# Keys and values of the next group at other places of a group's slots, and other places for the steps behind the projection, in an attention and mixture-of-experts kernel

## Chip, cores and metric

The kernel runs on one core of a Trainium2 chip. The metric is the device time of one execution in microseconds (us). Before the change it is 1366.93 us, the median of three runs (1366.15 to 1367.98).

## The reference

The input x is 8 sequences of 512 rows with 256 numbers each, all fp32. Two blocks follow each other, each inside a "sandwich" of two layer norms.

```
x = x + layernorm(attention(layernorm(x)))
x = x + layernorm(ffn(layernorm(x)))

attention: q = x @ wq + bq + pe      16 heads of 128: 4 groups of 4 heads
           k = x @ wk + bk + pe      one key head for each group
           v = x @ wv + bv           one value head for each group
           softmax(causal(q @ k.T / sqrt(128))) @ v, then @ wo

ffn:       softmax over 64 experts, the 6 best of each row, at most 64 rows for each expert,
           silu(rows @ w_gate) * (rows @ w_up) @ w_down, weighted and summed;
           plus one shared expert on all rows
```

Mean and variance of a layer norm are over the 256 numbers of a row.

## The kernel before

**Units and slots.** The attention is cut into 128 units: 8 sequences ("batches"), 4 groups of heads, 4 units for a group. Unit k holds two blocks of 64 queries for each of the group's four heads, one from the first half of the sequence and one from the second, four score tiles in all. A loop over k (L1520) writes the work of all engines in order; what one pass of the loop issues is called slot k here. b = k // 16 is the batch and s = k % 16 the slot within it; "first" to "fourth" slot means k % 4 = 0 to 3. The order on each engine is the order in which the program issues (a manual schedule): an instruction that waits holds up all that is behind it on its engine, and a DMA that waits holds up all that is behind it in the queue of the engine that issues it. Two such queues matter here, that of SyncE (SP) and that of GpSimd (POOL).

**What a slot does.** `scores(k, q)` (L571) multiplies queries by the keys kt of the group (TensorE, PE: psc, L580), VectorE (DVE) adds the mask and finds the extreme (L584), ScalarE (ACT) takes the exponential with its sum (L588). `weigh(k)` (L591) takes the reciprocal on DVE (recip, L594) and scales on POOL (e, L598). In the next slot `turned` (L612) transposes the weights in blocks of 32 on DVE (eb, L616), writes them to DRAM by four DMAs of SP (ex_d, L620), and `read_turned` (L625) reads them back in another order (et, L629): this completes the transposition. Two slots after the scores `mix` (L652) multiplies them by the values v (pav, L665). In the second slot of each group it does four units' remaining products in banks called rest and more (L704), and for units of a second slot the read of et is issued after it (L1590), in other slots early.

**Queries.** Pairs of heads are made by a product with seven factors instead of eight (`ask` L479, `ask_sum`, `answer`, `ask_rest`, `ask_fourth`, `answer_fourth`): banks pq_front and pq_back in the first and third slots, "third" (L527) in the second and fourth.

**Keys and values of the next group.** `keys` (L374) is a product of two weights tiles with 512 columns (pk, L378), and DVE adds bias and positions (kt, L380). `values(b, g, n)` (L382) makes half n of the values (pv, L390), which ACT copies to v, and for n = 0 in part to w as well. `group_step(k)` (L399) says when: keys in the second slot, half 0 of the values in the third, half 1 in the fourth. It is called at the end of a slot (L1632), but for second slots up to unit 96 between `projections_behind` and `mix` (L1587), that is, right behind "third" and ahead of rest on PE. Slots 2 and 3 of batch 0 are special (L1582).

**Banks.** The score tiles, third, rest, more and some tiles of the feed-forward part share three PSUM banks (pool ps_s); pk, pv, pq, pav, psg, pg and others share three more (ps_m). A product waits until the last reader of the bank's former tile is done.

**The feed-forward part behind it.** While batch b is in the attention, the rows of batch b - 1 go through the output projection and the feed-forward part. `feed_forward(b - 1)` (L1260) gives a table of steps with a place each, a slot s and a side. In the order of a slot the sides are A and B behind `weigh`, with `projections` between them in some slots, M ahead of group_step and mix, and D at the end, ahead of the last call of group_step. Places such as "4M" are slot 4, side M. The steps that matter:
- copies: for batches 1 to 5 `combine` (L805) on POOL, six additions, gives o, the projected rows.
- scales(o), scales(xt): `norm_scales` (L84): four bn_stats, four bn_aggr and one addition on DVE, then a power on POOL (rs_o, rs_f).
- residual_sums: a shift on DVE from rs_o (L105), four scalings of o on ACT (L109), four additions to x on POOL (L1287); for batch 5 the scaling is on DVE.
- store: x to DRAM by POOL's queue (x_d, L1290).
- rows: the second layer norm into xg (DVE L118, ACT L109), turn: its transposition.

The rows of x live in two buffers, so the rows of batch b + 1 (`load_x`, L188, on SP's queue, issued behind the et read of slot 6) go where those of batch b - 1 were. Their moments (st_a) are taken in slot 7, normalised in slot 8. `cross` (L770), four additions on POOL, prepares a seven-factor product of the projection and is issued at the start and at the end of third slots; its products are ps and pc (L783).

Of the kernel before, what the change touches and what calls it, by code (L numbers as in the profile page):

```python
# [22 lines left out]
NI = T // P  # L23
# [22 lines left out]
LATE_UNITS = (EARLY + 1) * NH  # L46

@with_exitstack
def sandwich_kernel(ctx, tc, x, wq, bq_t, wkv, bk_t, bv, wo, gate_wt, w_gate, w_up, w_down,
# [107 lines left out]
    with ExitStack() as part:  # L157
# [216 lines left out]
        def keys(b, g):  # L374
            s = seqs[b]
            pk = bank([P, T], f"pk_{b}_{g}")
            for c in range(NC):
                nc.tensor.matmul(pk, lhsT=wkv_sb[:, c, g, 0, :], rhs=s["xnt"][:, c, :], start=c == 0, stop=c == NC - 1)  # L378
            kt = s["kt"][g] = p2.tile([D, T], F32, tag="kt", name=f"kt_{b}_{g}")
            nc.vector.scalar_tensor_tensor(kt, pk, bk_sb[:, g : g + 1], pe_sb, ALU.add, ALU.add)  # L380

        def values(b, g, n):  # L382
            s = seqs[b]
            if n == 0:
                s["v"][g] = p2.tile([P, NI, D], F32, tag="v", name=f"v_{b}_{g}")
                s["w"][g] = p2.tile([P, 2, D], F32, tag="w", name=f"w_{b}_{g}")
            pv = bank([P, 2, D], f"pv_{b}_{g}_{n}")
            for i in range(2):
                for c in range(NC):
                    nc.tensor.matmul(pv[:, i, :], lhsT=s["xnt"][:, c, ts(2 * n + i, P)], rhs=wkv_sb[:, c, g, 1, :],  # L390
                                     start=c == 0, stop=c == NC - 1, skip_group_check=True)
            on_act(s["v"][g][:, ts(n, 2), :], pv)
            if n == 0:
                on_act(s["w"][g][HALF:, :, :], pv[:HALF, :, :])
                on_act(s["w"][g][:HALF, 1, :], pv[HALF:, 0, :])
                if b > EARLY:
                    nc.gpsimd.memset(s["w"][g][:HALF, 0, :], 0.0)

        def group_step(k):  # L399

            b, n = divmod(k, NH)
            g, step = n // QPG + 1, n % QPG
            b, g = (b, g) if g < G else (b + 1, 0)
            if b == B:
                return
            if step == 1:
                keys(b, g)
            if step >= 2:
                values(b, g, step - 2)

        def units_of(k):
# [438 lines left out]
        def projections_behind(k):  # L850
            c = crossing(k)
            if c:
                add_up(c[0], 0)
                across(c[0])
# [194 lines left out]
        def gate_up(key):  # L1049
            l = pairs[key]  # L1050
            pgu = bank([P, 2, F], f"pgu_{key}")
            for c in range(2):
                for e in range(2):
                    nc.tensor.matmul(pgu[ts(e, CAP)], lhsT=l["gxt"][:, c, ts(e, CAP)],
                                     rhs=l["wgu"][:, e, :, c, :], start=c == 0, stop=c == 1)
            l["hid"] = p4[0].tile([P, F], F32, tag="xhid", name=f"hid_{key}", bufs=2)
            nc.scalar.activation(l["hid"], pgu[:, 0, :], AF.Tanh, scale=0.5)
            l["pgu"] = pgu

        def gate_up_hidden(key):  # L1060
            l = pairs[key]
            pgu = l.pop("pgu")
            nc.vector.scalar_tensor_tensor(l["hid"], l["hid"], 1.0, pgu[:, 0, :], ALU.add, ALU.mult)
            nc.vector.scalar_tensor_tensor(l["hid"], l["hid"], 0.5, pgu[:, 1, :], ALU.mult, ALU.mult)

        def turn_hidden(key):
            l = pairs[key]
            pt = ps_s.tile([P, 2, P], F32, tag="s", name=f"pth_{key}")
            cols = l["hid"].rearrange("s (p c) -> s c p", c=2)
            for c in range(2):  # L1070
                nc.tensor.transpose(pt[:FC, c, :], cols[:, c, :], ident)
            l["ht"] = p3.tile([FC, 2, P], F32, tag="ht", name=f"ht_{key}")
            on_dve(l["ht"], pt[:FC])
# [186 lines left out]
        def feed_forward(b):  # L1260
# [14 lines left out]
            def scales(src, name):  # L1275
                l["scales"] = norm_scales(tiles_of(src), f"{name}{b}")
# [42 lines left out]
            def go(which, n=1):  # L1319
                return lambda: [next(l[which]) for _ in range(n)]  # L1320

            steps = {
                "2D": copies, "3M": lambda: scales(l["o"], "o"), "4A": residual_sums,
                "5M": lambda: scales(xt, "f"), "5B": store, "6A": rows,
                "6M": turn, "7A": shared_gate, "7B": go("f"), "8A": gate,
                "8D": go("r"), "9D": go("r"),
            }
            def choice_behind(steps):
                choose, then = steps.pop("8D"), steps.get("9A", lambda: None)
                return steps | {"9A": lambda: (choose(), then())}  # L1330

            if b < B - 2:
                steps |= {"3D": steps.pop("2D"), "4M": steps.pop("3M"), "5A": steps.pop("4A"),
                          "5D": steps.pop("5M"), "6B": steps.pop("5B")}
            if b == B - 2:
                steps["6D"] = steps.pop("6M")
            if b < B - 2:
# [1 line left out]
            if b < EARLY:  # L1339
# [8 lines left out]
                steps = choice_behind(steps)  # L1348
# [15 lines left out]
            def down_late():  # L1364
# [3 lines left out]
            steps = choice_behind(steps) | {  # L1368
                "10A": go("r"), "10B": mark, "10D": gather_rows, "11D": lambda: gate_up("late"),
                "12A": lambda: gate_up_hidden("late"), "12D": lambda: turn_hidden("late"), "13A": down_late,  # L1370
            }
# [148 lines left out]
        for k in range(NK):  # L1520
# [61 lines left out]
            if k == 2:  # L1582
                group_step(2)
                group_step(3)
            projections_behind(k)
            if k % NI == 1 and k < LATE_UNITS:
                group_step(k)  # L1587
            if k >= 2:
                mix(k - 2)
            if 0 <= k - 1 < NK - 2 and k % NI == 1 and k <= LATE_UNITS + 1:  # L1590
# [25 lines left out]
            if s == 2 and b:  # L1616
                behind = feed_forward(b - 1)
# [10 lines left out]

            if s in ((6, 8, 9) if b == EARLY + 1 else (10,) if b <= EARLY else ()):
                next(ahead)()  # L1630
            if k not in (2, 3) and (k % NI != 1 or k >= LATE_UNITS):
                group_step(k)  # L1632
            twice = active and k > EARLY * NH + NH
            if twice and not finishing:
# [101 lines left out]
```

## Time and profile before

| what | value |
|---|---|
| median of 3 runs | 1366.93 us |
| the profiled execution | 1366.87 us |
| its span, first to last instruction | 1365.2 us |
| busy PE, DVE, POOL, ACT | 1312.4, 926.4, 662.5, 586.0 us |
| granted TensorE clock | 0.998 |
| batches 1 to 4 start at (PE, unit 16 b) | 145.3, 296.3, 446.6, 596.4 us |

The last row is the start of the first score product of each batch in the trace. A row of the waits names the engine, the tile and line that waited, who ended the wait, the total in us, how often, and the longest. A row of the timeline gives start and length in us, engine, line, operation, output and inputs, how many instructions are merged, and in brackets the idle time of that engine ahead of it with what ended it; DMA rows of a queue (SPq) are the times of issue. All matmuls are fp32 and each product of the code shows as two or more MATMUL records.

### The profile page before, as it was taken

The numbers are of one execution on the slowest core, as the hardware profiler recorded it, in microseconds if no ns is written. First come the engines' busy times: TensorE is split into PE (matmuls) and PEld (weight loads), VectorE is DVE, ScalarE is ACT, GpSimd is POOL, SyncE is SP. The second block draws the span as 40 slices with busy tenths as digits, with TensorE's granted clock in tenths as the row PEclk, the third lists the DMA queues.
The fourth block names the chain that finished last, engine by engine and source line by source line (L and its number), as shares of the span: only waits on it lengthen the run. The fifth ranks groups of instructions, "written<-read, shape, count | busy, mean of one in ns | idle before, by whom it ended". The sixth has DMA issues, their size and how long they took to land. (4 is left out here: it accounts for less than half of the span.)

```text
span 1365.2 us, 22004 instructions
## 1 busy us (share of the span) xinstructions
PE 1312.4 (96%) x6746; PEld 997.1 (73%) x6746; DVE 926.4 (68%) x2955; ACT 586.0 (43%) x1777; POOL 662.5 (49%) x1090
## 2 busy tenths in 40 slices
PE   8999999999899999999999999999999999999997
PEld 6777776877778876787678876877666676777774
DVE  5575677877787678777787769766656444567545
ACT  3444455344544454444534454433444344444423
POOL 4555453436543563446443554345545445477711
PEclk9999999999999999999999999999999999999999
DMA  8676667666666657675765656678999889777711
GB/s 265 176 228 206 201 173 223 200 201 199 184 217 203 194 178 231 187 224 166 212 201 176 195 179 192 187 219 279 307 287 284 249 241 303 177 243 260 212 38 71
DMA packets 160437, 285.54 MB, mean 209 GB/s; under 512 B 17292, under 2 KB 123437, under 8 KB 160317
## 3 DMA queue, kind: packets, MB, share of 16 engines
q1 hardware_dynamic: 122893, 212.14, 52.0%
q0 software_dynamic: 13328, 36.05, 8.8%
q10 hardware_dynamic: 24096, 35.92, 8.4%
q8 instruction: 55, 0.90, 0.3%
q14 instruction: 65, 0.53, 0.1%
HBM read 168.44 MB, written 115.61 MB: 208 GB/s over the span
## 5 line engine op out<-in xcount | busy, mean ns | idle before, releaser
L598 POOL TENSOR_SCALAR e<-e,recip 128x512 f32<-128x512 f32 (+1 forms) x504 | 245.0, 523 | 436.6 <-DVE recip L594 384.8
L588 ACT ACTIVATE e<-e,least 128x32 f32<-128x32 f32 (+1 forms) x504 | 258.5, 514 | 243.1 <-DVE least L584 223.3
L580 PE MATMUL psc<-kt,qt 128*128 128x32 f32 (+15 forms) x1024 | 274.8, 406 | 17.8 <-DVE least L584 10.8
L584 DVE CUSTOM_DVE_ANT_0 e<-psc,mask 128x32 f32<-128x32 f32 (+1 forms) x504 | 205.4, 430 | 110.9 <-PE psc L580 108.1
L665 PE MATMUL pav<-et,v 128*128 128x256 f32 (+1 forms) x1044 | 258.3, 387 | 18.0 <-DMA et<-ex_d 15.6
L665 PEld LDWEIGHTS pav<-et,v 128*128 128x128 f32 (+1 forms) x1044 | 190.3, 191 | 65.8 <-issue 21.1
L674 ACT ACTIVATE ao<-pav,bv_sb 128x256 f32<-128x256 f32 x207 | 89.4, 471 | 332.3 <-PE pav L665 313.6
L580 PEld LDWEIGHTS psc<-kt,qt 128*128 128x128 f32 x1024 | 162.2, 191 | 66.2 <-DVE least L584 31.8
L616 DVE STREAM_TRANSPOSE eb<-e 128x1024 f32<-128x1024 f32 (+1 forms) x252 | 197.6, 822 | 12.6 <-DMA ex_d<-eb 6.3
L588 ACT ACTIVATION_READ_ACCUMULATOR e<-e,least 128x1 f32 x504 | 94.3, 187 | 0.0
L1091 POOL DMA_INDIRECT y_d<-dd,idx x32 | 51.0, 1595 | 86.6 <-ACT e L588 39.5
L783 PEld LDWEIGHTS pc<-set,crossed 128*128 128x128 f32 x640 | 77.2, 192 | 3.1 <-POOL crossed L777 0.9
L783 PE MATMUL pc<-set,crossed 128*128 128x128 f32 x640 | 78.2, 275 | 0.0
L433 PE MATMUL pq<-xnt,wq_sb 128*128 128x256 f32 x320 | 75.5, 380 | 0.0
L477 PE MATMUL pq_back<-rows_joined,heads 128*128 128x256 f32 x264 | 71.3, 379 | 0.0
L390 PEld LDWEIGHTS pv<-wkv_sb,xnt 128*128 128x128 f32 x512 | 66.0, 192 | 5.8 <-ACT w L121 1.3
L390 PE MATMUL pv<-wkv_sb,xnt 128*128 128x128 f32 x512 | 67.7, 276 | 1.6 <-ACT w L121 1.1
L433 PEld LDWEIGHTS pq<-xnt,wq_sb 128*128 128x128 f32 x320 | 59.2, 190 | 9.9 <-issue 1.5
L783 PEld LDWEIGHTS ps<-set,ao 128*128 128x128 f32 x480 | 59.5, 192 | 8.0 <-issue 2.4
L477 PEld LDWEIGHTS pq_back<-rows_joined,heads 128*128 128x128 f32 x264 | 50.2, 190 | 16.2 <-issue 8.2
L378 PE MATMUL pk<-xnt,wkv_sb 128*128 128x512 f32 x128 | 60.2, 593 | 0.3 <-ACT xnt L121 0.3
L783 PE MATMUL ps<-set,ao 128*128 128x128 f32 x480 | 60.5, 276 | 0.0
(303 smaller groups left out, 2174.0 us busy)
## 6 DMA issues: line engine op xcount, KB each, us to landing
ex_d<-eb SPq DMA_DIRECT2D x504, 160.0 KB
et<-ex_d SPq DMA_DIRECT2D x126, 640.0 KB
wgu<-in_w_gate ACTq DMA_DIRECT2D x32, 352.0 KB
wgu<-in_w_up ACTq DMA_DIRECT2D x32, 352.0 KB
wd<-in_w_down ACTq DMA_DIRECT2D x32, 352.0 KB
set<-wc_d SPq DMA_DIRECT2D x20, 512.0 KB
set<-ws_d SPq DMA_DIRECT2D x20, 384.0 KB
y<-y_d POOLq DMA_DIRECT2D x10, 512.0 KB, 6.2
```

The costliest lines, as they stand in the source:

```text
L378: nc.tensor.matmul(pk, lhsT=wkv_sb[:, c, g, 0, :], rhs=s["xnt"][:, c, :], start=c == 0, stop=c == NC - 1)
L390: nc.tensor.matmul(pv[:, i, :], lhsT=s["xnt"][:, c, ts(2 * n + i, P)], rhs=wkv_sb[:, c, g, 1, :], start=c == 0, stop=c == NC - 1, skip_gro ...
L433: nc.tensor.matmul(pq[:, n, :, :], lhsT=wq_sb[g][:, c, ts(2 * pair + n, D)], rhs=seqs[b]["xnt"][:, c, :].rearrange("p (u v) -> p u v", v=P ...
L477: nc.tensor.matmul(out, lhsT=factor[0], rhs=factor[1], start=first, stop=last, skip_group_check=True)
L580: nc.tensor.matmul(psc[:, :w], lhsT=halves[k // 2][:, at, :, :].rearrange("d h t -> d (h t)"), rhs=seqs[b]["kt"][g][:, :w], start=True, st ...
L584: nc.vector.tensor_tensor_reduce(out=e, in0=psc[:, :w].rearrange("p (c t) -> p c t", t=BS), in1=mask[:, T - w :].rearrange("p (c t) -> p c ...
L588: nc.scalar.activation(e, e, AF.Exp, bias=l["least"][:, q : q + 1], scale=-1.0, accum_out=l["total"][:, q : q + 1])
L598: engine.tensor_scalar(e, e, recip[:, q : q + 1], 1.0, ALU.mult, ALU.mult)
L616: nc.vector.transpose(eb[:, :, first : first + count, :, :].rearrange("p a j r t -> p j a r t"), weighed[k % 2][:, end - count : end, :, : ...
L665: nc.tensor.matmul(out, lhsT=keys_, rhs=weights, start=first and at == 0, stop=last and at == len(some) - 1, skip_group_check=True)
L674: nc.scalar.activation(result_of(k, n), out, AF.Identity, bias=bias)
L783: nc.tensor.matmul(bank_[:, n, :], lhsT=a, rhs=w, start=pair == 0 and n == 0, stop=pair == 1 and n == len(factors[0]) - 1, skip_group_chec ...
```

## The change

`group_step`: for units 4 to 95 the steps within a group are mapped so that keys are made in the first slot, half 0 of the values in the second, nothing in the third, half 1 in the fourth, and every call is at the end of the slot. For the batches whose steps the second edit covers (steps of batches 0 to 5), scales(o) goes from 4M to 4A, residual_sums from 5A to 4M, scales(xt) from 5D to 5A, and store from 6B to 5B.

```diff
@@ group_step
             b, g = (b, g) if g < G else (b + 1, 0)
             if b == B:
                 return
+            if NI <= k < LATE_UNITS:
+                step = (1, 2, 0, 3)[step]
             if step == 1:
                 keys(b, g)
-            if step >= 2:
+            if 2 <= step <= 3:
                 values(b, g, step - 2)
@@ feed_forward
             if b < B - 2:
-                steps |= {"3D": steps.pop("2D"), "4M": steps.pop("3M"), "5A": steps.pop("4A"),
-                          "5D": steps.pop("5M"), "6B": steps.pop("5B")}
+                steps |= {"3D": steps.pop("2D"), "4A": steps.pop("3M"), "4M": steps.pop("4A"),
+                          "5A": steps.pop("5M")}
@@ the loop over k
             projections_behind(k)
-            if k % NI == 1 and k < LATE_UNITS:
-                group_step(k)
             if k >= 2:
                 mix(k - 2)
@@
-            if k not in (2, 3) and (k % NI != 1 or k >= LATE_UNITS):
+            if k not in (2, 3):
                 group_step(k)
```

## The prediction

> **What bounds the kernel now.** The page first. TensorE (PE) is busy in 96% of the span:
>
> ```profile
> span 1365.2 us, 22004 instructions
> ...
> PE 1312.4 (96%) x6746; PEld 997.1 (73%) x6746; DVE 926.4 (68%) x2955; ACT 586.0 (43%) x1777; POOL 662.5 (49%) x1090
> ```
>
> Its work is the same after the change, so only its idle time can go, 52.8 us in all. The view of the waits, for PE alone, says what ended it:
>
> ```profile
> PE pav L665 <- DMA et<-ex_d: 15.6, 16, 2.8
> PE psc L580 <- DVE least L584: 10.8, 12, 1.2
> PE psc L580 <- DVE qt L512: 6.4, 4, 1.7
> PE psg L1214 <- DVE qt L512: 3.3, 4, 1.0
> ...
> PE pav L665 <- DVE kt L380: 1.7, 4, 0.4
> ```
>
> The same view over batches 1 to 4 (145.3 to 746.9 us) gives 7.7 us in 8 waits for least, and all of the two qt rows and of the kt row: a pattern that returns in each batch. The timeline places it. I take batch 2, whose slots 4 to 10 start on PE at 328.85, 334.25, 343.68, 354.38, 365.02, 374.89 and 384.29:
>
> ```profile
> 334.03 1.89 POOL L598 TENSOR_SCALAR e<-e,recip 128x512 f32<-128x512 f32 x4 [4.46 <-DVE recip L594]
> ...
> 336.25 1.04 POOL L99 TENSOR_TENSOR rs_o<-ve_o,mhalf 128x4 f32<-128x4 f32 x1 [0.34 <-DVE ve_o L97]
> 336.39 1.02 PE L580 MATMUL psc<-kt,qt 128*128 128x448 f32 x2 [0.83 <-DVE least L584]
> ...
> 338.11 1.88 PE L378 MATMUL pk<-xnt,wkv_sb 128*128 128x512 f32 x4
> ...
> 342.11 2.78 POOL L1287 TENSOR_TENSOR x<-x,o 128x256 f32<-128x256 f32 x4
> ...
> 342.87 0.43 DVE L89 BATCH_NORM_STATS2 st_f<-x 128x6 f32<-128x256 f32 x1 [0.93 <-POOL x L1287]
> ...
> 346.12 0.59 PE L580 MATMUL psc<-kt,qt 128*128 128x384 f32 x1 [1.09 <-DVE least L584]
> ```
>
> Slot 4 is only 5.40 us of PE work, and DVE ends it with the moments of o; so in slot 5 PE waits 0.83 us for a bank that DVE has not read. At the end of slot 5 DVE waits 0.93 + 3 x 0.26 us for POOL's additions to x; so PE waits 1.09 in slot 6. Then the queues, each from the timeline of its engine (SP, POOL, DVE, PE):
>
> ```profile
> 352.19 0.34 SPq L629 DMA_DIRECT2D et<-ex_d  x1
> 358.22 0.40 SPq L188 DMA_DIRECT2D x<-in_x  x1
> 358.66 2.07 SPq L144 DMA_DIRECT2D exr_d<-xb_f  x4
> 360.77 2.87 SPq L620 DMA_DIRECT2D ex_d<-eb  x4
> ```
>
> ```profile
> 352.62 0.80 POOL L1290 DMA_DIRECT2D x_d<-x  x1
> ```
>
> ```profile
> 362.69 1.41 DVE L89 BATCH_NORM_STATS2 st_a<-x 128x6 f32<-128x256 f32 x4 [3.60 <-DMA x<-in_x]
> ...
> 366.87 1.57 DVE L616 STREAM_TRANSPOSE eb<-e 128x768 f32<-128x768 f32 x2 [0.92 <-DMA ex_d<-eb]
> ```
>
> ```profile
> 365.02 2.38 PE L580 MATMUL psc<-kt,qt 128*128 128x32 f32 x8 [1.60 <-DVE qt L512]
> ...
> 370.06 1.98 PE L1214 MATMUL psg<-xt,sg_sb 128*128 128x512 f32 x4 [0.94 <-DVE qt L512]
> ```
>
> This is one chain. The store of x (L1290) is issued at 352.62 and lands at 358.14; the next batch's rows go into that buffer, so their load stands at the head of SP's queue until 358.22, with eight writes behind it. DVE waits 3.60 us for the rows, reads the bank of "third" only after that, and PE loses 1.60 at the start of slot 8 and 0.94 within it.
>
> **The change part by part.** PE does the same instructions, so the gains and costs are waits. The sum is made against the profiled execution: 1366.87 us (span 1365.2 and 1.67 around it); the median of the runs is 1366.93, so 0.06 apart.
>
> *The store of x, from 6B to 5B.* On POOL it passes four cross operations and weigh(38). It follows rs_f: with the times found below, issue at 344.9, and with the same 5.5 us it lands near 350.5. The x load then waits for the last reads of x in slot 6 (351.9) and for the et read ahead of it, so it is issued near 352.4 instead of 358.22. It takes 4.4 us (358.22 to 362.6 before), to 356.8; DVE wants the rows when recip of slot 7 is done, near 358.4. Both waits of slot 8 go: 6.4 + 3.3 = **9.7 us** in batches 1 to 4. In batch 5 PE has no such wait.
>
> *Moments of o to 4A, additions to 4M, moments of x to 5A.* By hand from 333.95, where recip of slot 4 ends: moments of o 1.79 us to 335.74, gxt 0.34 to 336.1. Now shift_o needs rs_o, and POOL does that power behind weigh(36), which ends at 335.92: 1.04 us more, to 337.0. So DVE stands 0.95 us, a new wait, with kt and all scores of slot 5 queued behind. kt runs 337.15 to 337.85, and the first score is read at 338.1. PE starts slot 5 at 335.96 (1.71 later, for the keys) and needs that bank 1.31 later, at 337.27: a wait of 0.89 in place of 0.83. On ACT the four scalings run 337.25 to 339.3, on POOL the additions 337.9 to 340.7, while DVE gets to the moments of x only at 341.9. So DVE no longer waits there, is free at 344.5, and slot 6 starts on PE at 345.1: its wait goes, 4.4 us in batches 1 to 4 and 1.1 in batch 5, **5.5**.
>
> *Keys to the first slot, half of the values to the second.* Four matmuls, 1.71 us from start to start (338.11 to 339.82), leave the second slot for the first; eight of values, 0.89, leave the third for the second. DVE gets kt just before the scores of the second slot: in slot 13 of batch 2 kt starts 0.19 after the next PE work can start and takes 0.70. Then two scores (0.38) and the two transposes (1.49) bring DVE to the third score at S+2.76 (S is the slot's start), and its bank is free at S+3.4. PE wants that bank for "rest" right behind third, at S+2.76 (S+1.90 to pq_back, 0.43 for each of the two pairs), because the keys no longer lie between. A new wait of **0.6 us** where nothing else lies there: what hid it was the keys.
> - slot 5: rest is ready at 339.88, the bank at 340.35: 0.47; with the 0.06 above 2.7 in five batches, less 0.7 of et waits that it absorbs in batches 4 and 5: 1.9.
> - slot 1: 0.6 against 0.61, 0.04, 0.43, 0.31 and 0.26 of et wait, which it covers: 1.4.
> - slot 9: four transposes lie between, 0.05: 0.2. In slot 13 twelve py matmuls do: nothing.
> - batch 0, slots 5 and 9: 1.2, and in slot 8 of batch 5 keys would wait some 0.3 for the bank of pg.
>
> Bounds of this unknown: nothing, if DVE is 0.6 earlier, to the whole cover of 1.71 in each of 16 slots, 27 us. I take my working, nearest to the rows.
> Gained by the keys: pav no longer waits for the kt bank in slot 9 (1.7), and DVE's lateness in slot 9 of batch 0 (0.9) is covered by a longer slot 8.
>
> *Sum*: 9.7 + 5.5 + 1.7 + 0.9 = 17.8 gained; 1.9 + 1.4 + 0.2 + 1.2 + 0.3 = 5.0 lost. Net 12.8, so **1354 us**. Batch 6 has slots of 14 us and more, and I put it at nothing (bounds 1 either way).
>
> **Rivals.**
> 1. *DVE's lateness moves, and does not go.* If the new wait for rs_o or ACT's scalings take 1 us more, the moments of x wait for POOL again and slot 6 keeps its wait: 5.5 back, 1359.5. For it: three engines hand over within one short slot. Against: 1.2 us of room at 341.9.
> 2. *The x load still comes late.* Slot 8 keeps its 9.7: 1363.8. The early store now runs beside the et read of slot 6, and the load beside that of slot 7. Row: the last packet (5120 bytes) of the et read issued at 343.87, by itself, ends at 347.4 (3.6 us); of the one issued at 352.19, beside the store, at 356.5 (4.3 us), so 0.7 more; the rows of x have 1.6 us of room, et 2. The Trainium skill (DMA: Bandwidth & Descriptors, "Issuing engines are not separate DMA queues") says that transfers from SP, ACT and POOL share the same 16 engines and interleave; by that alone, 512 KB more ahead of the load eat most of the room. The trace agrees with the sharing, at 0.7 us.
> 3. *Slower: the keys' cover.* If DVE comes to the third score later than I work out, each of 16 second slots pays up to 1.71. The balance turns at 1.1 us in each, against 0.6; with all of it, 1366.9 - 17.8 + 27.4 = 1376.5. For it: in slot 1 of batch 3 the transposes waited 0.47 for POOL. Against: the longer first slot gives POOL 1.7 us more for just that.
> 4. *Better*: if rs_o is quick, slot 5 loses nothing, 1.36 x 5 = 6.8 more: 1347.
> That the change does not do what it says is out: the order of instructions shows the keys, the values and the steps moved as told, with equal counts.
>
> **Numbers.** Forecast (1350 to 1358.5) 0.52; better 0.08; rival 1 0.14; rival 2 0.08; nothing left 0.06; slower 0.12. 0.2% is 2.7 us, about what a measurement of this kernel can tell from no change. Rival 2 lies on that bound and is split, so faster 0.79, same 0.09, slower 0.12. Range 1347 to 1364; what lies above is some 0.18.
>
> **What would show it.** Right: the SP wait of L188 for x_d (29.1 us in 6 waits) near nothing; st_a without a wait for in_x; PE's waits for qt gone; in slot 5 still some 0.9 for least, and a new one of rest for DVE of about half a microsecond; DVE waiting about 1 us for rs_o ahead of shift_o. Wrong: PE idle of 1 us or more ahead of rest in slots 1, 5 and 9 (rival 3), st_f still waiting for x (rival 1), or psc in slot 8 still waiting for qt (rival 2).

## The result, and the profile after

| | before | this |
|---|---|---|
| median of 15 runs each | 1367.95 us (1364.74 to 1374.19) | 1363.06 us (1357.87 to 1367.67) |
| the profiled execution | 1366.87 us | 1360.43 us |
| its span | 1365.2 us | 1358.7 us |

The ratio is 0.996 (95%: 0.9945 to 0.9974): faster, by 4.9 us of the medians and 6.5 us of the spans. The forecast was 12.8.

The page of the kernel after shows the same PE work in a shorter span:

```profile
span 1358.7 us, 21971 instructions
...
PE 1315.8 (97%) x6746; PEld 993.1 (73%) x6746; DVE 922.1 (68%) x2955; ACT 585.4 (43%) x1777; POOL 663.7 (49%) x1090
```

The waits of PE after (us in total, times, longest):

```profile
PE pav L667 <- DMA et<-ex_d: 12.1, 10, 2.8
PE psc L582 <- DVE least L586: 4.0, 6, 0.8
PE rest L667 <- DVE least L586: 3.9, 13, 0.3
PE pk L378 <- ACT ao L676: 2.6, 4, 0.6
...
PE more L667 <- DVE hid L1232: 1.0, 1, 1.0
...
PE psg L1216 <- DVE qt L514: 0.5, 2, 0.4
```

Lines are two further down than before (psc is L582). Of the waits for qt (L514) only 0.5 us in 2 is left of 9.7 in 8, and that for least has gone from 10.8 to 4.0. Of the rows shown, three stand for waits that before did not have: rest, pk and more. The timeline of batch 2, slots 5 to 8, which begin on PE at 333.95, 343.03, 351.4 and 360.3, answers to the lines shown of before:

```profile
333.87 1.05 POOL L99 TENSOR_TENSOR rs_o<-ve_o,mhalf 128x4 f32<-128x4 f32 x1
...
334.95 0.16 DVE L105 SCALAR_TENSOR_TENSOR shift_o<-mv_o,rs_o 128x4 f32<-128x4 f32 x1 [0.94 <-POOL rs_o L99]
335.03 0.74 DVE L380 SCALAR_TENSOR_TENSOR kt<-pk,bk_sb,pe_sb 128x512 f32<-128x512 f32 x1
...
336.00 1.02 PE L582 MATMUL psc<-kt,qt 128*128 128x448 f32 x2 [0.74 <-DVE least L586]
...
338.18 0.70 PE L667 MATMUL rest<-et,w 128*128 128x256 f32 x2 [0.30 <-DVE least L586]
...
339.73 1.37 DVE L89 BATCH_NORM_STATS2 st_f<-x 128x6 f32<-128x256 f32 x4
...
343.03 2.00 PE L582 MATMUL psc<-kt,qt 128*128 128x160 f32 x8
```

DVE stands 0.94 us for rs_o, kt and the scores are late behind it, and PE loses 0.74 and then 0.30. But st_f no longer waits for POOL, and slot 6 starts its eight products without a gap. The queues in the same timeline:

```profile
342.76 0.80 POOL L1292 DMA_DIRECT2D x_d<-x  x1
...
350.49 0.34 SPq L631 DMA_DIRECT2D et<-ex_d  x1
351.00 0.40 SPq L188 DMA_DIRECT2D x<-in_x  x1
...
356.41 0.75 DVE L89 BATCH_NORM_STATS2 st_a<-x 128x6 f32<-128x256 f32 x2 [0.26 <-DMA x<-in_x]
```

The store is issued ten microseconds earlier than before. The load of x is issued 0.5 us behind the et read instead of 6 us behind it; the wait for x_d has gone from SP's view; DVE waits 0.26 us for the rows where it waited 3.60 (0.37, 0.80 and 0.84 in batches 1, 3 and 4).

So what the change was forecast to gain is there, and something else took half of it. To find it, I cut both traces into slots. A slot runs from the first score product of one unit on PE to that of the next. Where PE work was moved, I take it out: 1.71 us for the keys, 0.89 for half of the values (the start-to-start times of the prediction). What is left is lost or gained time. After minus before, in us:

| slots | batches | forecast | measured |
|---|---|---|---|
| 7 and 8 | 1 to 4 | -9.7 | -10.2 |
| 6 | 1 to 5 | -5.5 | -7.0 |
| 9 | 1 to 4 | -1.5 | -1.4 |
| 5 | 1 to 5 | +1.9 | +1.5 |
| 1 | 1 to 5 | +1.4 | +1.5 |
| all | 0 | +0.3 | -0.6 |
| 11, 12, 13 | 1 to 4 | 0 | **+4.7** |
| 0 | 2 to 5 | 0 | **+2.8** |
| 7 to 13 | 5 | +0.3 | **+2.75** |
| all | 6 and 7 | 0 | -0.6 |

The rows add up to the 6.5 us of the spans. Three rows, 10.2 us, carry the error. Nothing of them was in the forecast but 0.3 us in batch 5. The trace shows what each is.

*Slot 12.* The timeline of batch 2:

```profile
407.65 1.46 PE L667 MATMUL pav<-et,v 128*128 128x256 f32 x6
409.23 0.47 ACT L676 ACTIVATE ao<-pav,bv_sb 128x256 f32<-128x256 f32 x1 [3.91 <-PE pav L667]
409.75 1.98 PE L378 MATMUL pk<-xnt,wkv_sb 128*128 128x512 f32 x4 [0.65 <-ACT ao L676]
```

The keys come right behind pav, and they start when ACT has emptied pav's bank: ACT had been idle for 3.91 us, so the wait is nothing but pav's own end and one eviction. Before, with the keys in the second slot, the scores of slot 13, py, pq_back and third lay between pav and them, and behind pav the scores came without a gap:

```profile
413.60 1.46 PE L665 MATMUL pav<-et,v 128*128 128x256 f32 x6
414.90 2.06 PE L580 MATMUL psc<-kt,qt 128*128 128x96 f32 x8
```

*Slot 9 of batch 5.* Here the keys have been taken away from between third and rest:

```profile
825.51 0.59 PE L479 MATMUL third<-xnt,heads 128*128 128x256 f32 x2
...
825.94 0.59 PE L667 MATMUL rest<-et,w 128*128 128x256 f32 x2
...
827.43 0.69 DVE L1232 SCALAR_TENSOR_TENSOR hid<-gs,psu 128x512 f32<-128x512 f32 x1
...
828.17 0.48 PE L667 MATMUL more<-held,v 64*128 64x256 f32 x1 [1.00 <-DVE hid L1232]
```

`more` takes the bank of psu, which DVE reads for hid behind nine instructions of the routing. Before, the keys lay there, and their 1.71 us covered that; now PE stands 1.00. Before:

```profile
831.68 1.88 PE L378 MATMUL pk<-xnt,wkv_sb 128*128 128x512 f32 x4
...
834.46 0.38 PE L665 MATMUL more<-held,v 64*128 64x256 f32 x1
```

*Slot 0.* The timeline of batch 3, which begins at 441.70:

```profile
432.35 0.61 SPq L762 DMA_DIRECT2D set<-wc_d  x1
435.78 2.32 SPq L622 DMA_DIRECT2D ex_d<-eb  x4
...
442.10 0.34 SPq L631 DMA_DIRECT2D et<-ex_d  x1
442.49 0.53 SPq L315 DMA_DIRECT2D y_d<-zero_rest  x1
...
446.89 1.53 PE L667 MATMUL pav<-et,v 128*128 128x256 f32 x6 [1.19 <-DVE recip L596]
```

The row names recip, which ends at 446.78. Experiment 5 has pav start 0.91 us ahead of recip in the same slot, so it isn't waited for; in batch 2 the same wait is put down to et. The read of et is issued 0.40 us after the start of the slot; before, it was 0.35 ahead of it (the slot began at 446.60), and pav did not wait:

```profile
446.25 0.34 SPq L629 DMA_DIRECT2D et<-ex_d  x1
...
450.65 1.53 PE L665 MATMUL pav<-et,v 128*128 128x256 f32 x6
```

### The profile page after: what moved, and what is told of

Read it like the earlier page. It is cut to its first block, busy times and chain, and to the rows that moved or that the text cites. A ratio compares the mean times of both kernels' runs of the same rounds, so it can differ in the third digit from the quotient of the medians.

```text
span 1358.7 us, 21971 instructions
## 1 busy us (share of the span) xinstructions
PE 1315.8 (97%) x6746; PEld 993.1 (73%) x6746; DVE 922.1 (68%) x2955; ACT 585.4 (43%) x1777; POOL 663.7 (49%) x1090
## 5 line engine op out<-in xcount | busy, mean ns | idle before, releaser
L582 PE MATMUL psc<-kt,qt 128*128 128x32 f32 (+15 forms) x1024 | 276.1, 407 | 5.0 <-DVE least L586 4.0
L582 PEld LDWEIGHTS psc<-kt,qt 128*128 128x128 f32 x1024 | 160.8, 191 | 65.3 <-DVE least L586 28.7
L479 PEld LDWEIGHTS pq_back<-rows_joined,heads 128*128 128x128 f32 x264 | 50.2, 190 | 16.2 <-issue 8.2
```

The source lines that it names most:

```text
L479: nc.tensor.matmul(out, lhsT=factor[0], rhs=factor[1], start=first, stop=last, skip_group_check=True)
L582: nc.tensor.matmul(psc[:, :w], lhsT=halves[k // 2][:, at, :, :].rearrange("d h t -> d (h t)"), rhs=seqs[b]["kt"][g][:, :w], start=True, st ...
```

## The experiments

Each kernel ran beside runs of the kernel before on the same chip. Differences are of medians, against those runs (1367.68 us for experiments 1 to 4, 1365.66 for 5 to 8, 1366.98 for 9 to 12; 1367.95 beside the change). "By slots" means lengths adjusted as above, in the profiled execution. That is one run of several, and its difference from before can be up to 5 us off that of the medians (experiment 11): the slots say where time goes, the medians how much. Edits are against the kernel after, unless another is named; "..." stands for lines left out.

**1. The steps alone.** The kernel before, with the line of the steps from the change; keys and values as before. Against the kernel before:

```
-                steps |= {"3D": steps.pop("2D"), "4M": steps.pop("3M"), "5A": steps.pop("4A"),
-                          "5D": steps.pop("5M"), "6B": steps.pop("5B")}
+                steps |= {"3D": steps.pop("2D"), "4A": steps.pop("3M"), "4M": steps.pop("4A"),
+                          "5A": steps.pop("5M")}
```

> The steps of the change alone; keys and values stay where they were. Theory 1 (the steps gain about 17 us by the store that no longer holds the queue, and the moved keys and values give back about 10 of it through three waits of their own): slots 6 to 8 gain some 17 us as after the change, but the new wait of DVE for rs_o is no longer covered by a longer slot 4, so slot 5 loses about 1.1 us in five batches; no wait of pk for ACT in slot 12, none of rest in slot 1. 10 to 13 us under the kernel before, so 5 to 8 under the change. Rival (the new wait of DVE for rs_o is what costs, and the moved keys are a gain that covers it): no faster than the change, 0 to 5 us under the kernel before.

1353.8 us, 13.9 under before; ratio 0.9893 (0.9873 to 0.9914). The steps alone gain nearly three times what the whole change gains, a little more than expected. The moved keys and values are a loss.

**2. Keys and values alone.** The line of the steps as before:

```
-                steps |= {"3D": steps.pop("2D"), "4A": steps.pop("3M"), "4M": steps.pop("4A"),
-                          "5A": steps.pop("5M")}
+                steps |= {"3D": steps.pop("2D"), "4M": steps.pop("3M"), "5A": steps.pop("4A"),
+                          "5D": steps.pop("5M"), "6B": steps.pop("5B")}
```

> Keys and values moved as in the change, steps where they were. Theory 1: slower than before by 2 to 6 us: slot 12 loses 0.9 in four batches, slot 0 up to 1.2, second slots some 0.5, against 0.4 gained in slot 9 and some in slot 5. Rival (the moved keys are a gain): 3 to 6 us faster than before.

1386.2 us, 18.5 over before; ratio 1.0136 (1.0115 to 1.0158). Slower as said, but by far more: the two parts do not add (18.5 - 13.9 would be 4.6 over before, and the change is 4.9 under it). The timeline of its batch 2, slots 7 and 8:

```profile
358.74 0.80 POOL L1292 DMA_DIRECT2D x_d<-x  x1
...
364.37 0.40 SPq L188 DMA_DIRECT2D x<-in_x  x1
...
369.12 1.41 DVE L89 BATCH_NORM_STATS2 st_a<-x 128x6 f32<-128x256 f32 x4 [4.80 <-DMA x<-in_x]
...
371.45 4.05 PE L582 MATMUL psc<-kt,qt 128*128 128x32 f32 x8 [2.80 <-DVE qt L514]
```

It is the old chain, longer: slots 5 and 6 are shorter by the moved PE work, POOL's work ahead of the store is not. The load comes 4.8 us into slot 7, where it was 3.8, and DVE waits 4.80 for it, not 3.60. And there is more than the wait: the eight scores behind it take 4.05 us, where the same scores before took 2.38. The granted clock was 0.5 for 3.4 us from 371.6. In each of batches 1 to 4 it fell so, within or behind idle times of PE of 4.32, 2.80, 2.08 and 3.11 us (in batch 1 for 6.8 us), and at no other time ahead of batch 7; before, it was 1.00 throughout batches 0 to 6. PE is busy for 14.7 us of these stretches, so an estimate of the loss is half of that, some 7 us. Slots 7 and 8 of batches 1 to 4 are 8.9 us longer than before, while PE's waits for qt there have grown by 2.6 only, from 9.7 to 12.3. With the new steps there is no such chain to lengthen, and no such idle time; that is why the parts don't add.

**3. The store alone.** The kernel before, with nothing but the store in place 5B. Against the kernel before:

```
-                          "5D": steps.pop("5M"), "6B": steps.pop("5B")}
+                          "5D": steps.pop("5M")}
```

> Only the store of x moves, from 6B to 5B; all else as before. Theory 1: the SP wait for x_d falls from 5.6 us to about nothing in each batch and slots 7 and 8 together lose their waits, 2.5 us in each of batches 1 to 4: 9 to 11 us under the kernel before. Rival (DVE's lateness moves on and the queue is not what sets the pace): the SP wait goes, but less than 4 us of time with it.

1355.29 us, 12.4 under before; ratio 0.9912 (0.9894 to 0.993). By slots 7 and 8 of batches 1 to 4 are 10.8 us shorter, and slot 6 is no shorter (0.2 longer). That step of the prediction stands by itself. The medians differ by a little more than the 9 to 11 expected.

**4. Keys and values moved in groups 1 and 2 alone** (slots 4 to 11), with the new steps:

```
+        def early(k):
+            return NI <= k < LATE_UNITS and 4 <= k % NH < 12
...
-            if NI <= k < LATE_UNITS:
+            if early(k):
                 step = (1, 2, 0, 3)[step]
...
```

The lines left out call `group_step` for the other second slots where the kernel before does.

> The change, but keys and values are moved only in slots 4 to 11; in slots 0 to 3 and 12 to 15 they stay where they were. Theory 1: the waits in slots 12, 13, 0 and 1 go (3.7 + 0.5 + 2.8 + 1.5 us by the lengths of the slots in the two traces), so 7 to 9 us under the change, 12 to 15 under the kernel before. Rival 3 of the prediction in a milder form (the loss is the uncovered rest of the second slots everywhere): only slot 1 comes back, 1 to 2 us under the change.

1351.46 us, 16.2 under before and so 11.3 under the change; ratio 0.9877 (0.9855 to 0.9899). In batch 2 slots 12 and 13 lose 0.00 by slots, slot 11 0.12, and slot 0 gains 0.5. By slots it is 8.8 us under the change, within the 7 to 9 expected; the 11.3 of the medians is more. What the change lost in these slots comes almost all from the other two groups.

**5. The keys alone** (with the new steps; half 0 of the values stays in the third slot):

```
-                step = (1, 2, 0, 3)[step]
+                step = (1, 0, 2, 3)[step]
```

> The change as it is, except that half of the values stays in the third slot; only the keys are in the first. Theory (three separate losses): the wait for et at the start of batches 2 to 5 comes from a third slot that is 0.89 us shorter, so it goes (2.8 us less than the change), while the keys' waits for ACT in slot 12 (0.65 us, four times) and those of rest in the second slots stay. 1 to 4 us under the change. Rival (one cause: the longer first slot shifts everything behind it): the waits for et stay, and the time is that of the change within 1 us.

1355.47 us, 10.2 under before, 5.3 under the change; ratio 0.9915 (0.989 to 0.9941). Slot 12 keeps its 0.92 us in each of batches 1 to 4, and slot 0 of batches 2 to 5 loses nothing (-0.06 to 0.01). Batch 3, which begins at 441.95 here:

```profile
441.01 0.34 SPq L631 DMA_DIRECT2D et<-ex_d  x1
441.40 0.53 SPq L315 DMA_DIRECT2D y_d<-zero_rest  x1
...
445.94 1.56 PE L667 MATMUL pav<-et,v 128*128 128x256 f32 x6
```

The read is issued 0.94 ahead of the slot. So slot 0's loss is that of the values, and slot 12's that of the keys. In batch 5 the keys keep slots 8, 9 and 13 (0.41, 1.32, 0.51). By slots it is 3.5 us under the change, within the 1 to 4 expected; the medians say more.

**6. Half of the values alone**, the keys in the middle of the second slot:

```
-                step = (1, 2, 0, 3)[step]
+                step = (0, 1 if keyed else 2, 0, 3)[step]
...
+            if k % NI == 1 and k < LATE_UNITS:
+                group_step(k, True)
...
```

> The change as it is, except that the keys stay in the second slot, where they were; only half of the values is moved. Theory: the wait of the keys for ACT in slot 12 goes (4.2 us by slot lengths), the waits of rest in slots 1, 5 and 13 go, and the wait for et at the start of batches 2 to 5 stays; the gain in slot 9 (1.4) goes too. 4 to 8 us under the change. Rival (the keys cost nothing, the values all): as slow as the change or slower.

1357.86 us, 7.8 under before, 2.9 under the change; ratio 0.9931 (0.9908 to 0.9954). Slot 12 is as before (0.00), the waits of rest are gone, slot 0 keeps its loss (1.49, 0.61, 0.00 and 1.11). It gains less than expected because of slot 5, which I had not put in: +4.8 us in batches 1 to 5, against +1.5 in the change. The early keys put off the start of slot 5 by 1.71 us, and that covered a part of DVE's stand for rs_o; with the keys late, slot 5 pays more of it (in the steps alone too: 3.9). Slot 11 has its 0.13 us in each of batches 1 to 4 here and not in experiment 5: that is the values', too.

**7. The zeros elsewhere.** The whole change, with the writes of zeros (L315, 15 in all, from the late slots of batches 1 to 3) in slots 3 to 7:

```
-            if k in (2, NH) or 1 <= b < EARLY and s >= 11:
+            if k in (2, NH) or 1 <= b < EARLY and 3 <= s <= 7:
```

> The change as it is, with the writes of zeros to y_d in batches 1 to 4 in slots 3 to 7 and not in 11 to 15. Theory: the et read ahead of slot 0 is late because the ex_d writes come sooner after the shorter third slot and meet the zeros and the loads of sets on the DMA engines; without the zeros the wait of pav for et in slot 0 shrinks from 0.2 to 1.3 us to near nothing, 2 to 3 us less there. Rival (the shorter third slot alone leaves the read too little time): slot 0 keeps its wait within 0.2 us. The zeros may cost something in slots 6 to 8, beside the load of x, under either.

1364.77 us, 0.9 under before; ratio 0.9986 (0.997 to 1.0002): 4.0 us worse than the change. By slots, slot 0 of batches 2, 3 and 4 falls from 0.79, 1.15 and 0.22 to 0.00, 0.22 and 0.01, and that of batch 5, ahead of which no zeros are written in either kernel, stays (0.62 and 0.69). Slot 8 of batches 1 to 3 gets 3.9 us worse: the zeros now meet the load of x, for which DVE waits 7.9 us in 6 waits, against 4.6 in 6 in the change. Batch 3, beginning at 443.68:

```profile
443.99 0.34 SPq L631 DMA_DIRECT2D et<-ex_d  x1
...
447.95 1.53 PE L667 MATMUL pav<-et,v 128*128 128x256 f32 x6 [0.26 <-DVE gxt L505]
```

The read is issued 0.31 after the start, nearly as late as in the change, but pav has its data within 3.96 us of it, against 4.79 with the zeros behind the read. The packets of the read in the two traces say the same: the last one ends 4.0, 4.4 and 3.7 us after the issue in batches 2, 3 and 4 of the change, and 3.6, 3.5 and 3.6 here. So both theories hold a part: the moved values make the read late, in all four batches, and the zeros make it long, by 0.4 and 0.8 us in two of them. Why it is late is argued, not isolated: in the change the set load comes 0.9 us nearer to the ex_d writes than before (432.35 against 435.78; 436.34 against 440.69), and from the first of the writes to the read it takes 6.3 us, not 5.6. With the keys alone the distance is that of before, and it takes 5.0. A rival stands beside it: POOL issues a write of 512 KB (y_d<-y) 0.5 us ahead of the set load, so it comes nearer to the writes by as much.

**8. Groups 1 and 2 in batches 0 to 4.** Experiment 4 without batch 5. Against experiment 4:

```
-            return NI <= k < LATE_UNITS and 4 <= k % NH < 12
+            return NI <= k < 5 * NH and 4 <= k % NH < 12
```

> The steps, with keys and half values moved in slots 4 to 11 of batches 0 to 4 alone; batch 5 has them where they were. Theory: what slots 7 to 11 of batch 5 lose (1.9 us with the keys moved there) comes from the keys and values of that batch and goes: 13 to 16 us under the change, 1 to 3 under the kernel with groups 1 and 2 moved in all batches (1351.5 then). Rival (batch 5 loses because it begins later against transfers issued at fixed times): no difference from that kernel.

1350.13 us, 15.5 under before, 10.6 under the change; ratio 0.9876 (0.9852 to 0.9899). By slots, slots 7 to 13 of batch 5 lose 0.00, so their loss is that of the keys and values made there. The medians (16.2 and 15.5 under before) do not tell this kernel from experiment 4, where these slots lose 2.2; only the slots do. My 13 to 16 under the change was too much.

**9. Experiment 8, with shift_o, scalings and additions behind two scores of slot 5.** This is aimed at the 0.94 us that DVE stands for rs_o. Against experiment 8:

```
-                steps |= {"3D": steps.pop("2D"), "4A": steps.pop("3M"), "4M": steps.pop("4A"),
+                steps |= {"3D": steps.pop("2D"), "4A": steps.pop("3M"), "5S": steps.pop("4A"),
...
             scores(k, 3)
             scores(k, 2)
+            side(s, "S")
```

> The kernel with keys and half values moved in slots 4 to 11 of batches 0 to 4 and the new steps, and shift_o, scalings and additions issued behind the first two scores of slot 5 instead of in the middle of slot 4. Theory (PE's wait in slot 5 is DVE's wait of 0.94 us for rs_o, with kt and the scores queued behind it): psc no longer waits for least in slot 5, which becomes 0.5 to 1.0 us shorter in batches 1 to 5, 3 to 5 us in all, and the additions still end before the moments of x are wanted: 1345 to 1348 beside 1366 of the kernel before. Rival (the additions come 0.5 us later and the moments of x wait for them): slot 6 gets back up to 1.4 us, and the time stays within 1 us of the kernel without the move.

1347.24 us, 19.7 under before; ratio 0.985 (0.9828 to 0.9872). By slots, slot 5 is 3.9 us shorter than in experiment 8 over batches 1 to 5, as expected; slot 8 gives back 2.6. All slots of these batches together leave 2.1, so the 4.2 us between the two experiments' medians are more than the slots account for.

**10. The whole change with that edit.** The same two places are edited, in the kernel after.

> The whole change, with shift_o, scalings and additions behind the first two scores of slot 5. Theory: 3 to 5 us under the change, all of it in slot 5 (0.5 to 1.0 us shorter in batches 1 to 5); slots 0, 12 and those of batch 5 keep what they lose. Rival: within 1 us of the change.

1361.05 us, 5.9 under before and only 1.0 under the change; ratio 0.995 (0.9932 to 0.9968). The median is the rival's, the slots are the theory's: slot 5 is 4.05 us shorter over batches 1 to 5 and slot 8 is 2.6 us longer over batches 1 to 4. The timeline of batch 2 says why:

```profile
333.80 2.20 PE L582 MATMUL psc<-kt,qt 128*128 128x96 f32 x8
335.05 0.16 DVE L105 SCALAR_TENSOR_TENSOR shift_o<-mv_o,rs_o 128x4 f32<-128x4 f32 x1
...
339.24 1.37 DVE L89 BATCH_NORM_STATS2 st_f<-x 128x6 f32<-128x256 f32 x4
...
351.05 0.40 SPq L188 DMA_DIRECT2D x<-in_x  x1
...
356.97 1.41 DVE L89 BATCH_NORM_STATS2 st_a<-x 128x6 f32<-128x256 f32 x4 [1.77 <-DMA x<-in_x]
```

The eight scores of slot 5 run without a gap, nothing waits for rs_o, and the moments of x don't wait for the additions: the rival's mechanism is wrong. But DVE now wants the rows of x 0.95 us sooner, and their load, behind the et read in SP's queue, is issued when it was (351.05, 351.00): 1.77 us instead of 0.26.

**11. The steps alone with that edit.** The same two places are edited, in the kernel of experiment 1.

> The steps alone (keys and values where they were before), with shift_o, scalings and additions behind the first two scores of slot 5. Here kt is issued in slot 5 behind them in any case, so only the scores are freed of the wait for rs_o. Theory: slot 5 0.5 to 1.0 us shorter in batches 1 to 5 (it was 0.4 to 1.0 longer than before), 3 to 5 us under the steps alone. Rival: within 1 us of the steps alone.

1347.87 us, 19.1 under before, 5.2 more than the steps alone gain; ratio 0.9863 (0.984 to 0.9885). Slot 5 is 4.9 us shorter by slots over batches 1 to 5, slot 6 gives back 0.40 in batch 2 and next to nothing elsewhere, slot 8 nothing. This and experiment 9 are the best of all kernels here and beat both the kernel before and the change; from each other they can't be told. Without moving any keys or values one is there.

**12. Keys and values with the early store**, the other steps as before. Against experiment 2:

```
-                          "5D": steps.pop("5M"), "6B": steps.pop("5B")}
+                          "5D": steps.pop("5M")}
```

> Keys and values moved as in the change, and of the steps only the store of x in 5B instead of 6B (moments and additions stay where they were before). Keys and values alone, with the late store, had lost 18.5 us. Theory (half of that is the late store's chain, pushed further by the longer first slot; the rest is what the keys and values lose by themselves in slots 0, 12 and batch 5): the waits of psc for qt in slot 8 go, and the time is 14 to 20 us under keys and values alone, 0 to 4 us under the kernel before. Rival (the loss is the keys and values' own, the store has no part in it): only the 12 us that the early store gains by itself come off, or fewer: 5 us or more above the kernel before.

1366.95 us; ratio 1.0001 (0.9987 to 1.0015): the same as before. It is 18.5 us better than keys and values with the late store, 6 us more than the early store gains without them (12.4): so much came of the longer chain and of the half clock behind it, which this kernel does not have (its clock is 0.5 only from 1359.7 us on). And it is 12.4 worse than the store alone (experiment 3): that is what the moved keys and values cost by themselves, without the new places for the moments and the additions. With these it is 13.9 - 4.9 = 9.0.

## Why the prediction was right in sign and too large

- *The store of x.* Right, in size too: 9.7 forecast, 10.2 measured, and 10.8 with the store alone. SP no longer waits for x_d. The load took longer than the 4.4 us I put: 351.00 to 356.41 is 5.4. It was also issued 0.7 us later than forecast, counted from the start of slot 6 (343.03, forecast 345.1), and DVE was ready 0.2 sooner. Rival 2's margin of 1.6 us was thus used up, with 0.26 us of wait in batch 2 to show for it, and 1.77 in experiment 10. Over the kernel 4.6 us of such waits are left of 19.0: "st_a without a wait for in_x" did not come true. That the median of 1363.06 us stands next to rival 2's 1363.8 is chance: slot 8 did not keep its 9.7. What is cited there, from the Trainium skill (DMA: Bandwidth & Descriptors, "Issuing engines are not separate DMA queues"), is that transfers interleave on the same 16 engines whichever engine started them. The trace agrees: the last packet of the et read of slot 6, on SP's queue, ends 4.4 to 4.6 us after its issue in batches 1 to 4 with POOL's store issued 0.2 to 0.5 us behind it, and 3.5 to 3.7 before, without the store.
- *Moments and additions.* Right: shift_o waits 0.94 for rs_o (forecast 0.95), psc 0.74 (0.89), st_f no longer for x, and slot 6 gains 7.0, not 5.5: the row of 1.09 us that goes stands for 1.40 of slot. Rival 1, that the wait moves and does not go, did not happen.
- *Slots 1, 5 and 9.* Right within 0.4 us: rest waits 0.30 in the row, where 0.47 and 0.6 were put.
- *The keys in slot 12: the first step that failed.* "Four matmuls, 1.71 us from start to start, leave the second slot for the first": the forecast priced this where the keys were taken from and not where they land. "In slot 13 twelve py matmuls do: nothing" was nearly so (0.13), but in slot 12 the keys stand right behind a product whose bank they need: 0.92 us in each of four batches, 4.2 in all with slot 13 (experiment 5). That is a wait in the place of none, and what it comes from could be read in the trace of before: pav, then psc, in slot 12, with no other product between.
- *The values: the second.* "Eight of values, 0.89, leave the third for the second": priced at nothing where they leave. With them gone from the third slot the et read of slot 0 is issued 0.6 to 1.6 us later than before, and slot 0 lost 2.8 (experiments 5 and 6); slot 11 lost 0.5. That the third slot's length had kept the transfers ahead of that read apart from the writes is my reading of it, and not shown.
- *Batch 5: the third.* "In slot 8 of batch 5 keys would wait some 0.3" was nearly so (0.41), but slots 7 to 13 lost 2.75, nearly half of it (1.33) in slot 9, where keys had covered DVE's reading of the banks behind the routing. The keys lost 2.2 of it (experiment 5), the values 0.5 (experiment 6). This is rival 3's mechanism, the keys' cover, in a place where I had not looked for it. I had worked it through for third's bank in slots 1, 5, 9 and 13, and not for `more`.
- *The sum.* The gains, 17.8 in the forecast, came to 19.8, of which 1.2 are in batches 0, 6 and 7, where much varies from kernel to kernel; the losses, 5.0, came to 13.3. Rival 3 had the sign of the keys and values right (experiments 1, 2, 3 and 12), though not of the change.

What stays open: the cause of the late et read is argued from the distance to the set load, and no run moved that load, or POOL's write beside it. Why the clock falls behind some idle times of PE and not behind others is open too. Slots 6 to 14 of batch 7 vary between kernels by up to 4 us where nothing in their code differs (a stretch of 3.4 us at half clock stands in some of them and not in others), so differences of 2 to 3 us between spans say little, and I rest on slots of batches 0 to 5.

## What to carry to other kernels

When a full engine's work is moved, price both ends: what the moved block covered where it was, for every bank and read behind it, and what the instruction ahead of it holds where it lands. Compare two kernels slot by slot with the moved work taken out; a total that looks like a small gain can be a large gain and a large loss. And once a transfer no longer waits, what stands ahead of it in its queue sets when it is issued: in experiment 10, DVE was ready sooner and only waited longer for it. When two parts of a change don't add, look for what one of them lengthens for the other, and look at the clock in that stretch too.

## What the runs showed of the hardware

- A gap in PE's row can be less than what is lost. For pk in slot 12 the row says 0.65 us and the slot is 0.92 longer, with no wait there before. The profile's ends of matmuls are modelled, and here the next product starts ahead of them where nothing waits: before, pav ended at 415.06 by its row and psc started at 414.90.
- Half a megabyte of x took 4.2 to 4.6 us (batches 1 to 4) with the 640 KB read of et issued 6 us ahead of it, 5.4 to 6.1 when issued 0.5 us behind that read, and 5.8 to 6.3 in experiment 10. The distance is not all: in batch 1 of experiment 2 it took 6.3 in spite of 6 us.
- 176 KB of zeros issued 0.4 us after the read of et made it 0.4 and 0.8 us longer in batches 2 and 3, and 0.1 in batch 4 (experiment 7).
- In experiment 2 the granted clock was 0.5 for 3.4 us or more within or behind idle times of PE of 2.08 to 4.32 us, and eight scores took 4.05 us instead of 2.38. This is no rule: in batch 7 of the change PE stands 2.79 and 2.10 us and the clock stays at 1.00.
